# Deformable layer beside a state-space scan: the scan's preparation in bank 2, lower weights in SBUF, state rows issued in a tile's second slot

## The chip, the core and the metric

The kernel runs on one core of one Trainium2 chip. The metric is device time in microseconds of one execution. The five engines are named as in the profile: PE (matmul; PEld its weight loads), DVE (vector), ACT (scalar), POOL (GpSimd) and SP, which here only issues DMAs. The kernel divides PSUM into eight tiles of 128 x 512 float32, called banks below.

## What is computed

Four residual layers over a batch of four images of 128 channels by 128 x 128 pixels, in float32, each behind a group norm:

```
x = x + deformable_conv(gn(x))     # offsets and mask from a 3x3 conv, bilinear samples, 9 taps
x = x + dilated_conv_chain(gn(x))  # 5x7 conv, two 1x1
x = x + state_space_block(gn(x))   # layer norm, projections, a scan in four directions, gate
x = x + central_difference_conv(gn(x))
```

Two parts matter here. The deformable layer samples each of nine taps at a computed place, as a weighted sum of four neighbours, and multiplies by a 128 x 128 matrix:

```
sampled = (corner(y0, x0, (1-ly)*(1-lx)) + corner(y0, x0+1, (1-ly)*lx)
         + corner(y0+1, x0, ly*(1-lx)) + corner(y0+1, x0+1, ly*lx)) * mask
out = einsum('bckhw,ock->bohw', sampled, weight)
```

The scan runs, for each of four directions, 128 channels and 16 states, along all 16384 pixels:

```
h = h * exp(delta * A) + (delta * u) * B
y = einsum('bkcn,bkn->bkc', h, C)
```

## The kernel before

**Two streams.** The program is written as Python generators. `scan` is the main stream: 512 tiles t (4 images x 4 directions x 32 blocks of 512 pixels). `together` draws a side stream beside it: for each scanned image the end of the image before (`layer2_post`, `layer3`) and the start of the next (`layer0_table`, `layer0`, `layer1`, `layer2_pre`), so that each side step comes at a fixed share of the scan's steps. The first image's `layer0` runs alone, the last stretch has no `layer0`: three of the four runs of `layer0` stand beside the scan. `keep_order` then fixes the written order of instructions on every engine, so what is issued early or late is decided in the Python text.

**A scan tile.** A tile has four parts j of four scans g, 16 slots. For each j, `inputs` multiplies du by the state rows into h (L936; on DVE the rows come from the PSUM tile dub, which `states_up`, L929, makes by a matmul; on POOL from an SBUF tile bb), `decay` makes exp(delta * A) on ACT into a PSUM tile pa (L966), L1079 is the scan on DVE, `carry_on` (L997) keeps the last column, `outputs` (L1003) multiplies h by cb, and `sums` (L977) adds up over states by matmul into yacc, which `finish` copies out and stores. While `layer0` runs beside it (`beside["busy"]` is "POOL"), all four inputs and all outputs are on DVE, otherwise the outputs and one input are on POOL.

**Preparation.** `prepare(t + 2)` is a generator drawn once a slot through `more` (three or four times in a part j). It makes three PSUM tiles, pdt, pxbc and psum, a chain of ACT instructions, delta and, on POOL, du (L908), and stores both to DRAM, from where they are spread over partitions.

**PSUM.** Four banks are the scan's: dub, two pa and yacc. Four are the side's: bank0 to bank3. In `layer0`, bank 0 holds the output sums acc (L510), banks 1 and 3 alternate for the transposed samples pst (L490), bank 3 serves the positions of the next strip while `got["third"]` is set, and bank 2 holds wl, the weights of the lower two neighbours. Where the side leaves bank 3 free (`beside["spare"]`, all other stages), the scan owns it: `own` is true, preparation's tiles lie in it, and a third pa when no preparation is under way. Beside `layer0`, `own` is false and preparation shares the one dub bank with the state rows.

**The deformable layer's weave.** Its unit n is a block of 512 pixels and a tap, 288 an image. `gather(n)` issues four indirect DMAs on POOL (L447) of 128 rows of 2 KB, and one POOL multiply of an earlier unit (L455). Two units later, ACT weighs the upper neighbours (L468) and DVE the lower ones, `weigh_lower`, two instructions L479 a unit; PE transposes and adds the four neighbours into pst (L490), ACT copies it to smp (L502), PE projects (L510), DVE adds the residual (L517). `positions` (L359 to L420) is drawn once a unit by `look` for the next strip of four blocks, and `lower_weights` makes wl once a strip (L428).

Of the kernel before, what the change touches and what calls it, by code (L numbers as in the profile page):

```python
# [10 lines left out]
F32 = mybir.dt.float32  # L11
# [7 lines left out]
P = 128  # L19
# [4 lines left out]
N = R * W  # L24
NBLK = H // R
KK = 9
# [5 lines left out]
NG = 4  # L32
# [8 lines left out]
ROWS = 16  # L41
# [71 lines left out]
def conv_preact_kernel(ctx: ExitStack, tc: tile.TileContext, a: dict, nb: int):  # L113
    nc = tc.nc
# [5 lines left out]
    pss = ctx.enter_context(tc.tile_pool(name="scps", bufs=1, space=PSUM))  # L120
# [7 lines left out]
    def bank(which, name):  # L128
        return psb.tile([P, N], F32, name=name, tag=f"bank{which}")

    waiting = []
    beside = {}
# [179 lines left out]
    def layer0(st, pairs=10):  # L312
# [5 lines left out]
        with ExitStack() as s:  # L318
# [6 lines left out]
            mp = s.enter_context(tc.tile_pool(name="l0m", bufs=1))  # L325

            got = {}
# [9 lines left out]
            def positions(j):  # L337
# [4 lines left out]
                y0 = j * ROWS  # L342
                xs, base, top = got["s", j]

                got["third"] = True
                po = bank(3, "po")
                po3 = po.rearrange("p (r w) -> p r w", w=W)
# [76 lines left out]
            def lower_weights(j):  # L424

                wts = got.pop(("l", j))
                wl = bank(2, "wl")[:, 0 : 2 * ROWS * KK]
                nc.vector.tensor_mul(  # L428
                    wl.rearrange("p (q n) -> p q n", q=2),
                    wts[:, 1:2, 0].to_broadcast([P, 2, ROWS * KK]), wts[:, :, 1],  # L430
                )
                got["p"] = wl.rearrange("p (q r b k) -> p r b k q", q=2, r=R, b=BPS)
# [105 lines left out]
                yield None  # L538
            flush()
            beside["full"] = True  # L540
            while beside.get("own") or beside.get("third"):
                yield None
            fetch_strip(0)
            for n, _ in enumerate(positions(0)):
# [6 lines left out]
                yield share + (1.0 - share) * f  # L551
            flush()
            beside["full"] = False
        st["x1"], st["stats1"] = keep, stats_out


# [260 lines left out]
    def scan(pull):  # L817
# [4 lines left out]
        seq = []  # L822
# [30 lines left out]
        def prepare(t, early=False):  # L853

            st, k, i, back = seq[t]
            c = blocks[t]
            if (st["b"], k) not in carries:
                carries[st["b"], k] = carry = small.tile([P, NST], F32, name="carry")
                nc.vector.memset(carry, 0.0)
            c["carry"] = carries[st["b"], k]  # L860
            c["bc"] = st["bc"][k % 2][i, k // 2]
            u = c["u"]
            own = beside.get("own")
            beside["prepares"] = own

            def place(name):
                return bank(3, name) if own else pss.tile([P, N], F32, name=name, tag="dub")

            yield None
            if own:  # L870
                yield None
            pdt = place("pdt")
            nc.tensor.matmul(pdt, wd[:, k, :], u, start=True, stop=True)
            yield None

            dtb = col(V_DTB + k)
            e = sp.tile([P, N], F32, name="e", bufs=1)
            nc.scalar.activation(e, pdt, AF.Abs, bias=dtb)
            above = sp.tile([P, N], F32, name="above", bufs=1)
            nc.scalar.activation(above, pdt, AF.Relu, bias=dtb)  # L880
            yield None
            nc.scalar.activation(e, e, AF.Exp, scale=-1.0)
            yield None
            one_e = sp.tile([P, N], F32, name="one_e", bufs=1)
            nc.scalar.activation(one_e, e, AF.Identity, bias=1.0)
            yield None
            if not back:
                px = place("pxbc")
                nc.tensor.matmul(px, xbc[:, k, :], u, start=True, stop=True)
            ln = sp.tile([P, N], F32, name="ln", bufs=1)  # L890
            nc.scalar.activation(ln, one_e, AF.Ln)
            yield None
            if not back:
                bc = sp.tile([4 * NST, N], F32, name="bc", bufs=1)
                nc.scalar.copy(bc, px[0 : 4 * NST])  # L895
                store(st["bc"][k][i].rearrange("d j s t -> (d j s) t"), bc)
            nc.scalar.activation(one_e, one_e, AF.Identity, bias=minus)  # L897
            yield from slots(1 if own else 2 if early else 4)
            pd = place("psum")
            for n, (t, sign) in enumerate(((e, ident), (one_e, less), (ln, ident), (above, ident))):  # L900
                nc.tensor.matmul(pd, sign, t, start=n == 0, stop=n == 3)  # L901
            yield from slots(1 if early else 2)
            steps = sp.tile([P, 2, N], F32, name="steps", bufs=1)
            delta, du = steps[:, 0, :], steps[:, 1, :]
            nc.scalar.copy(delta, pd)  # L905
            beside["prepares"] = False
            yield from slots(2 if early else 1)
            nc.gpsimd.tensor_mul(du, delta, u)  # L908
            c["steps"] = sd = dram.tile([P, 2 * N], F32, name="stepsd", bufs=4)
            store(sd, steps.rearrange("p j t -> p (j t)"), 2)  # L910
# [14 lines left out]
        def states_up(t, j):  # L925

            c = blocks[t]
            c["pb", j] = p = pss.tile([P, N], F32, name="dub", tag="dub")
            nc.tensor.matmul(p, xb[:, seq[t][1], j, :], c["u"], start=True, stop=True)  # L929
# [22 lines left out]
        def decay(n):  # L952

            t, n = divmod(n, NST)
            j, g = divmod(n, NG)
            k = seq[t][1]
            turn = (ahead["turn"] + 1) % 3
            if turn == 2 and (not beside.get("own") or beside.get("prepares")):
                turn = 0
            ahead["turn"] = turn  # L960
            if turn == 2:
                beside["third"] = beside.get("third", 0) + 1
                blocks[t]["third", n] = True
            pa = bank(3, "pa3") if turn == 2 else pss.tile([P, N], F32, name="pa", bufs=2)
            at = g * NG + j
            nc.scalar.activation(pa, blocks[t]["d", g], AF.Exp, scale=neg_a[:, k, at : at + 1])  # L966
            blocks[t]["a", n] = pa
# [54 lines left out]
        for t, (st, k, i, back) in enumerate(seq):  # L1022
            c = blocks[t]
            carry = c["carry"]
            on_vector = beside.get("busy") == "POOL"
            own = beside["own"] = bool(beside.get("spare")) and not beside.get("full")
            c["by"] = nc.vector if on_vector else nc.gpsimd
            more = prepare(t + 2, on_vector) if t + 2 < len(seq) else iter(())
            if t > 0:
# [1 line left out]
            for j in range(NG):  # L1031
# [16 lines left out]
                for g in range(NG):  # L1048
                    n = j * NG + g
                    if g == 1:  # L1050
                        decays(at + 1)
                        if t + 1 < len(seq) and j == 3:
                            spread_steps(t + 1, 2)
                            spread_steps(t + 1, 3)
                        if t + 1 < len(seq) and j == (2 if c["by"] is nc.gpsimd else 3):
                            spread_products(t + 1)
                        next(more, None)
                        if before[0] >= 0:
                            carry_on(*before, c["by"])
                            outputs(*before, c["by"])  # L1060
                        if earlier[0] >= 0 and not own:
                            sums(*earlier)
                        if own and j == 2 and t > 0:
                            finish(t - 1)
                    if n and g in (0, 3):
                        next(more, None)
                    if g == 3 and not own and then[0] < len(seq) and not (then[1] == NG - 1 and c["by"] is nc.gpsimd):
                        states_up(*then)
                    if g == 2:
                        decays(at + 2)  # L1070
                        if j == 0 and c["by"] is nc.gpsimd:
                            inputs(t, NG - 1, nc.gpsimd)
                        next(more, None)
                        if own and then[0] < len(seq) and not (then[1] == NG - 1 and c["by"] is nc.gpsimd):
                            states_up(*then)
                    o, f = h[:, g, :], c["a", n]
                    if back:
                        o, f = o[:, ::-1], f[:, ::-1]
                    nc.vector.tensor_tensor_scan(o, f, o, carry[:, n : n + 1], ALU.mult, ALU.add)  # L1079
                    if ("third", n) in c:  # L1080
                        beside["third"] -= 1
                    if g == 3:
                        decays(at + 3)
                        if own and earlier[0] >= 0:
                            sums(*earlier)
                        if not own and j == 1 and t > 0:
                            finish(t - 1)
                    yield (t * NST + n + 1) / total
            for _ in more:
                pass  # L1090
        t = len(seq) - 1
# [422 lines left out]
```

## Time and profile before

| what | us |
|---|---|
| median of 3 runs (20785.77 to 20800.34) | 20786.91 |
| the profiled execution, its own time | 20838.75 |
| its span, from the first to the last instruction | 20837.0 |
| gathers alone, first image (217 to 1930) | 1713 |
| gathers beside the scan (3446 to 5309, 8625 to 10443, 13537 to 15356) | 1863, 1818, 1819 |

Busy time of each engine in some stretches, from the trace:

| stretch, us | PE | DVE | ACT | POOL |
|---|---|---|---|---|
| 217 to 1930 (1713) | 1048.80 | 434.35 | 740.46 | 1288.72 |
| 3446 to 5309 (1863) | 1434.60 | 1645.09 | 1227.41 | 1540.28 |
| 8625 to 10443 (1818) | 1356.92 | 1438.83 | 1146.39 | 1488.65 |
| 13537 to 15356 (1819) | 1372.55 | 1434.63 | 1146.43 | 1488.93 |
| 5330 to 8570 (3240) | 2622.91 | 3036.56 | 2164.35 | 2799.78 |
| 10470 to 13500 (3030) | 2487.29 | 2824.51 | 2033.41 | 2567.93 |

How to read profile lines: a group's line gives the source line, engine, operation, output<-input by the program's names, shapes and count; then its busy time in us and the mean of one in ns; then the engine's idle time just before these instructions and what ended it. "issue" means that the profile shows nothing that the engine waited for. In order of time a line gives start, length, engine, line, operation, and in brackets the idle time before it. Small gaps between POOL's instructions are not counted as busy.

### The profile page before, as it was taken

To read this page: it belongs to the slowest core of one execution; us is meant where nothing else is said; L and a number is where in the kernel's file an instruction comes from. 1 tells how busy PE (TensorE), PEld (TensorE's weight loads), DVE (VectorE), ACT (ScalarE), POOL (GpSimd) and SP (SyncE) were. 2 spreads that over 40 slices of the span, in tenths; PEclk is the share of its full clock that TensorE was granted. 3 is DMA by queue.
4 is the path that set the end of the run, shared out by engine and by line. 5 is a ranking of instruction groups with operands and counts; after the bars stand their busy time and mean duration, and the time that the engine had idled before them with its cause. 6 is when DMAs were issued, how large, how long until landed. Compare 5 with 4: busy or idle time off the path is not lost.

```text
span 20837.0 us, 209864 instructions
## 1 busy us (share of the span) xinstructions
PE 15847.0 (76%) x58778; PEld 6719.5 (32%) x58778; DVE 16855.7 (81%) x14665; ACT 12887.2 (62%) x25086; POOL 16827.5 (81%) x10597
## 2 busy tenths in 40 slices
PE   4667776777878888777778887877777877677778
PEld 2444222444322223344422222244432222122223
DVE  1222588888999899888899889978889998999983
ACT  3444566666667666566667776666666767655563
POOL 4775577888788888888878888888878889999994
PEclk7888888998989999899999998988998988899899
DMA  7666678777767877777777796777776777555673
GB/s 234 192 193 191 193 229 283 259 255 253 245 205 225 235 236 254 239 247 251 247 235 224 225 250 229 253 244 248 248 241 221 235 216 221 185 185 195 197 219 120
DMA packets 2909354, 4717.50 MB, mean 226 GB/s; under 512 B 1095248, under 2 KB 1369240, under 8 KB 2831264
## 3 DMA queue, kind: packets, MB, share of 16 engines
q1 hardware_dynamic: 2539552, 3495.83, 52.5%
q0 software_dynamic: 368640, 1208.25, 18.8%
q8 instruction: 476, 7.80, 0.1%
q14 instruction: 686, 5.62, 0.1%
HBM read 3766.27 MB, written 908.60 MB: 224 GB/s over the span
## 4 chain that ended last, share of the span: by engine, by line
DVE 34%; PE 19%; issue 12%; DMA 11%; ACT 10%; POOL 8%; another core or an unknown queue 3%; SPq 2%; DVEq 0%; POOLq 0%; ACTq 0%
DVE h L1079 20%; DVE h L936 11%; PE pst L490 4%; PE psum L901 4%; POOL g L447 3%; DMA du<-stepsd 3%; ACT pa L966 3%; DMA g<-table,idx 2%; PE acc L510 2%; ACT g L468 2%; DMA delta<-stepsd 2%; PE p L1309 1%; POOL h L1003 1%; PE yacc L977 1%
## 5 line engine op out<-in xcount | busy, mean ns | idle before, releaser
L1079 DVE TENSOR_TENSOR_SCAN h<-pa,carry,h 128x512 f32<-128x512 f32 x8192 | 10005.1, 1267 | 767.6 <-ACT pa L966 571.5
L966 ACT ACTIVATE pa<-delta,neg_a 128x512 f32<-128x512 f32 x8192 | 5538.0, 687 | 4751.5 <-DVE h L1079 3700.4
L1003 POOL TENSOR_TENSOR h<-h,cb 128x2048 f32<-128x2048 f32 x1692 | 7670.5, 4533 | 137.0 <-POOL carry L997 0.6
L447 POOL DMA_INDIRECT g<-table,idx x4608 | 4874.2, 1058 | 1679.5 <-issue 1136.4
L936 DVE TENSOR_TENSOR h<-du,dub 128x2048 f32<-128x2048 f32 x1625 | 3684.3, 2267 | 826.4 <-PE dub L929 310.3
L490 PE MATMUL pst<-ident,g 128*128 128x128 f32 x18432 | 2670.0, 299 | 1665.1 <-issue 644.8
L929 PE MATMUL dub<-u,xb_sb 128*128 128x512 f32 x3250 | 2047.3, 716 | 1713.3 <-DVE h L936 1529.8
L490 PEld LDWEIGHTS pst<-ident,g 128*128 128x128 f32 x18432 | 2312.0, 155 | 2699.8 <-issue 1297.6
L468 ACT ACTIVATE g<-g,wt 128x128 f32<-128x128 f32 x8072 | 2577.6, 392 | 216.7 <-DMA g<-table,idx 162.4
L977 PE MATMUL yacc<-h,gather_sb 128*32 128x512 f32 x16384 | 2364.6, 650 | 87.0 <-POOL h L1003 61.0
L936 POOL TENSOR_TENSOR h<-du,bb 128x2048 f32<-128x2048 f32 x423 | 1927.4, 4557 | 18.1 <-DMA du<-stepsd 18.1
L479 DVE TENSOR_TENSOR g<-g,wl 128x512 f32<-128x512 f32 x2304 | 1488.2, 669 | 359.9 <-DMA g<-table,idx 315.4
L502 ACT COPY smp<-pst 128x512 f32<-128x512 f32 x1152 | 664.8, 577 | 1569.9 <-remote 1013.2
L929 PEld LDWEIGHTS dub<-u,xb_sb 128*128 128x128 f32 x3250 | 598.4, 210 | 2877.1 <-DVE h L936 2211.9
L510 PE MATMUL acc<-smp,w_sb 128*128 128x512 f32 x2304 | 1371.3, 679 | 133.2 <-DVE x L517 60.9
L908 POOL TENSOR_TENSOR steps<-steps,u 128x512 f32<-128x512 f32 x512 | 652.5, 1274 | 909.5 <-ACT steps L905 905.2
L1309 PE MATMUL p<-xn,w_l_sb 128*128 128x508 f32 (+2 forms) x2304 | 1149.6, 620 | 1.8 <-ACT xn L1288 1.8
L977 PEld LDWEIGHTS yacc<-h,gather_sb 128*32 128x32 f32 x16384 | 338.3, 112 | 1838.1 <-issue 1315.9
L901 PE MATMUL psum<-e,ident 128*128 128x512 f32 x1024 | 613.8, 684 | 357.6 <-ACT bc L895 338.0
L901 PE MATMUL psum<-one_e,less 128*128 128x512 f32 x1024 | 639.1, 711 | 310.7 <-ACT one_e L897 310.1
L517 DVE TENSOR_TENSOR x<-acc,xres 128x512 f32<-128x512 f32 x128 | 87.1, 680 | 966.5 <-remote 525.3
L455 POOL TENSOR_SCALAR g<-g,wt 128x128 f32<-128x128 f32 x1144 | 833.0, 728 | 37.4
(170 smaller groups left out, 18122.0 us busy)
## 6 DMA issues: line engine op xcount, KB each, us to landing
cb<-bcd SPq DMA_DIRECT2D x512, 1024.0 KB
delta<-stepsd SPq DMA_DIRECT2D x2048, 256.0 KB
du<-stepsd SPq DMA_DIRECT2D x2048, 256.0 KB
stepsd<-steps SPq DMA_DIRECT2D x512, 512.0 KB
table<-gt SPq DMA_DIRECT2D x512, 256.0 KB
bb<-bcd SPq DMA_DIRECT2D x512, 256.0 KB
win<-nd SPq DMA_DIRECT2D x512, 160.0 KB
g<-table,idx POOLq DMA_INDIRECT x4608
```

The costliest lines, as they stand in the source:

```text
L447: nc.gpsimd.indirect_dma_start(out=g[:, r].rearrange("p q c -> p (q c)"), out_offset=None, in_=table, in_offset=bass.IndirectOffsetOnAxis( ...
L468: nc.scalar.activation(g, g, AF.Copy, scale=w)
L479: nc.vector.tensor_mul(g, g, wl.unsqueeze(3).to_broadcast([P, 2, 2, P]))
L490: nc.tensor.matmul(pst[:, r * P : (r + 1) * P], g[:, r % 2, q, :], ident, start=q == 0, stop=q == 3, is_transpose=True,)
L510: nc.tensor.matmul(got["a", i], w0[:, k, :], got.pop(("c", n)), start=k == 0, stop=k == KK - 1)
L901: nc.tensor.matmul(pd, sign, t, start=n == 0, stop=n == 3)
L929: nc.tensor.matmul(p, xb[:, seq[t][1], j, :], c["u"], start=True, stop=True)
L936: engine.tensor_mul(h, c["du"], b.unsqueeze(1).to_broadcast([P, NG, N]))
L966: nc.scalar.activation(pa, blocks[t]["d", g], AF.Exp, scale=neg_a[:, k, at : at + 1])
L977: nc.tensor.matmul(c["y"][g * Q : (g + 1) * Q, :], gather, c["h", j][:, g, :], start=j == 0, stop=last and not second,)
L1003: engine.tensor_mul(h, h, c["cb"][:, j, :].unsqueeze(1).to_broadcast([P, NG, N]))
L1079: nc.vector.tensor_tensor_scan(o, f, o, carry[:, n : n + 1], ALU.mult, ALU.add)
```

## The change

Four edits belong together. `lower_weights` puts wl into an SBUF tile of the pool `mp` instead of bank 2. `own` becomes a number: 3 where the scan owns bank 3, 2 beside `layer0` (then preparation's tiles lie in bank 2), 0 otherwise; `beside["prepares"]` is now set at the start of each tile, and the third pa is allowed only where `own` is 3. Where `own` is 2, `states_up` for the next part comes in the second slot (g 1), after preparation's step, instead of the fourth; as `own` is true there now, `sums` and `finish` take the places that they have in the other stages. And `layer0` waits at its end until a preparation in bank 2 is through, and, where `positions` takes bank 3, first copies out the transposed samples that are still in a bank.

```diff
@@ positions
+                for n in [key[1] for key in got if key[0] == "t" and isinstance(key, tuple)]:
+                    copy(True)(n)
                 got["third"] = True
                 po = bank(3, "po")
@@ lower_weights
                 wts = got.pop(("l", j))
-                wl = bank(2, "wl")[:, 0 : 2 * ROWS * KK]
+                wl = mp.tile([P, 2 * ROWS * KK], F32, name="wl")
@@ layer0
-            while beside.get("own") or beside.get("third"):
+            while beside.get("own") == 3 or beside.get("third"):
                 yield None
...
             flush()
             beside["full"] = False
+            while beside.get("own") == 2 and beside.get("prepares"):
+                yield None
@@ prepare
             def place(name):
-                return bank(3, name) if own else pss.tile([P, N], F32, name=name, tag="dub")
+                return bank(own, name) if own else pss.tile([P, N], F32, name=name, tag="dub")
@@ decay
-            if turn == 2 and (not beside.get("own") or beside.get("prepares")):
+            if turn == 2 and (beside.get("own") != 3 or beside.get("prepares")):
                 turn = 0
@@ scan
-            own = beside["own"] = bool(beside.get("spare")) and not beside.get("full")
+            own = beside["own"] = 2 if beside.get("full") else 3 if beside.get("spare") else 0
+            beside["prepares"] = own if t + 2 < len(seq) else 0
...
                         next(more, None)
+                        if own == 2 and then[0] < len(seq):
+                            states_up(*then)
                         if before[0] >= 0:
...
-                        if own and then[0] < len(seq) and not (then[1] == NG - 1 and c["by"] is nc.gpsimd):
+                        if own == 3 and then[0] < len(seq) and not (then[1] == NG - 1 and c["by"] is nc.gpsimd):
                             states_up(*then)
```

## The prediction

> **What bounds the kernel now.** I read the page's head first, then the busy times by stretch, then the groups by line inside the one kind of stretch that the diff touches, and last the order of time there on two engines. The profiled execution took 20838.75 us (span 20837.0). The runs shown have a median of 20786.91, 0.25% less, so I work out a difference in the profiled execution and add it to the median.
>
> ```profile
> span 20837.0 us, 209864 instructions
> PE 15847.0 (76%) x58778; PEld 6719.5 (32%) x58778; DVE 16855.7 (81%) x14665; ACT 12887.2 (62%) x25086; POOL 16827.5 (81%) x10597
> ```
>
> No engine is full on average, so the share says little and the stage must be read. The gathers of L447 mark the deformable layer: they run from 217 to 1930 us alone, and beside the scan from 3446 to 5309, 8625 to 10443 and 13537 to 15356 us, three stretches of 1863, 1818 and 1819 us. Between them DVE is busy 3037 of 3240 us (5330 to 8570): the scan's engine is the bound there. In the gathers' stretches it is not: DVE 1439 of 1818. The groups of 8900 to 10300 us, 1400 us from the middle of such a stretch, tell who is:
>
> ```profile
> L447 POOL DMA_INDIRECT g<-table,idx x885 | 961.7, 1087 | 242.9 <-issue 198.7 <-ACT g L468 7.2 <-DVE g L479 6.6
> ...
> L479 DVE TENSOR_TENSOR g<-g,wl 128x512 f32<-128x512 f32 x445 | 290.1, 667 | 51.8 <-DMA g<-table,idx 40.5 <-issue 10.9
> ...
> L1003 DVE TENSOR_TENSOR h<-h,cb 128x2048 f32<-128x2048 f32 x84 | 196.6, 2341 | 2.9
> L936 DVE TENSOR_TENSOR h<-du,dub 128x2048 f32<-128x2048 f32 x83 | 189.6, 2285 | 180.6 <-PE dub L929 53.8 <-issue 44.4 <-remote 33.7
> L455 POOL TENSOR_SCALAR g<-g,wt 128x128 f32<-128x128 f32 x221 | 166.3, 753 | 7.3
> ...
> L908 POOL TENSOR_TENSOR steps<-steps,u 128x512 f32<-128x512 f32 x21 | 26.8, 1276 | 0.0
> ```
>
> Add POOL up: 961.7 + 242.9 + 166.3 + 7.3 + 26.8 = 1405 of 1400 us (the ends overlap). The 242.9 us are 885 gaps of 0.27 us, each 0.30 us between two gathers or 0.17 after a multiply: POOL's own pace, not a wait. Gaps longer than that add only 1, 7 and 8 us in the three stretches. **POOL is full beside the scan**, and nobody makes it wait. DVE's 180.6 us ahead of L936, where it waits for PE's state rows, is time that POOL hides.
>
> Now why a gather has a mean of 1087 ns where its median is 949. POOL, then DVE, in order of time (start, length, engine, line):
>
> ```profile
> 9518.79 1.02 POOL L447 DMA_INDIRECT g<-table,idx  x1 [0.16 <-issue]
> ...
> 9522.64 2.98 POOL L447 DMA_INDIRECT g<-table,idx  x1 [0.30 <-issue]
> ...
> 9536.86 2.74 POOL L455 TENSOR_SCALAR g<-g,wt 128x128 f32<-128x128 f32 x1
> ```
>
> ```profile
> 9518.13 2.29 DVE L936 TENSOR_TENSOR h<-du,dub 128x2048 f32<-128x2048 f32 x1 [11.03 <-remote]
> ...
> 9522.50 2.29 DVE L1003 TENSOR_TENSOR h<-h,cb 128x2048 f32<-128x2048 f32 x1
> ...
> 9536.91 2.29 DVE L1003 TENSOR_TENSOR h<-h,cb 128x2048 f32<-128x2048 f32 x1
> ```
>
> L1003 and L936 have the same shape and length. L1003 reads two SBUF tiles, and each time the POOL instruction that starts under it is about 2 us longer, a gather (2.98) or a multiply (2.74). L936 has one input in PSUM, and the gather under it keeps its 1.02. So a DVE instruction with **both inputs in SBUF** holds up the POOL instruction that starts under it. In the stretch the held time is 885 x (1087 - 949) ns + 221 x (753 - 624) ns = 150.6 us, less 13 us for the first gather after a multiply (221 x 0.06): 137 us over 84 L1003, **1.64 us each**. L479 does not do it today: its wl lies in PSUM.
>
> **The change, part by part.**
>
> *wl moves from bank 2 to SBUF.* L428 and L479 keep their number (576 of L479 for each of four images) and length (row L1003 against L936: 2341 and 2285 ns, the same within 56 ns). But L479 now has two SBUF inputs, like L1003. Its price is POOL time. The starts show the rule to use: a gather that began before the DVE instruction isn't held, one that begins under it ends 0.83 us after it, that is 0.12 us of its 0.95 are done by then. An instruction of 0.667 us so holds for about 0.52 us; POOL starts five instructions in a group of 5.58 us (four gathers, one multiply); with starts at random the mean hold is 5 / 5.58 x 0.52 squared / 2 = 0.12 us. The same sum for L1003 (2.13 us less 0.57, the mean time to the next start) gives 1.56 against 1.64 measured. So 576 x 0.12 x 1.05 = 73 us an image is one end. The other: laying L479's recorded intervals over POOL's recorded starts, with what L1003 already holds kept, POOL grows by 42 to 59 us in a stretch as recorded, and by 23 to 56 if DVE is stretched by 2 to 6% against it. I take 50, since L479 often sits next to an L1003 that has held POOL already: **3 x 50 = +150 us** (69 to 219).
>
> The Trainium skill, "SBUF — State Buffer", section "Who interferes with whom", speaks against this part: a DVE instruction with two SBUF inputs contends with a GpSimd one that reads SBUF, and whoever comes second blocks fully. The L1003 rows agree on the block (2.98 against 0.95 us). Read as if every L479 cost POOL its whole length, that is 576 x 0.667 x 3 = +1150 us; the starts above say that most L479 fall between two POOL starts.
>
> *The same in the first image's layer, alone.* There POOL is less full: 1110.4 + 179.0 us busy, and 102 us of its gaps in 1700 are longer than its pace, since it also waits for buffers and landings. The replay gives 48 to 66 us; those waits can take up part or all. I take **+30** (0 to 66).
>
> *The scan's preparation gets bank 2 (own is 2), state rows come at g 1 instead of g 3, sums and finish move two or more slots later.* No instruction is added and no DMA: one matmul pair (x166 for 83 rows) moves up, four sums by four matmuls move down, finish and its store by SP move from tile 1's last to tile 2's second slot, so one 256 KB store goes past a few loads in SP's queue; its reader is a later direction, many blocks off. pdt and the pair after it come a slot later, psum, delta and L908 in the same slots as now, so POOL's multiply of the steps isn't later. What goes away is PE's and DVE's wait about the dub bank (53.8 + 44.4 us in 1400). POOL hides it: **0**. If POOL's cover were gone this would be worth up to the 180.6 us of the row, or some 235 us a stretch; that is rival one. At each edge of a stretch POOL stands some 30 us (30.3 to 34.2 before the first gather, waiting for idx), of which a freer PE may save a few: **-10** (0 to -60, which takes the 1 + 7 + 8 us of gaps in).
>
> *The early copies when positions start.* A copy moved up inside its step, seven times an image, on ACT, busy 1146 of 1818: 0, at most 7 x 0.58 us x 3 = 12 if PE's waiting were bare.
>
> *The third decay bank.* "prepares" is now set at a tile's start, not at its second scan. Only decays 1 and 2 of a tile could lose bank 3. Counting turns: after nine alternating decays the cycle puts the third bank at decays 13 and 16 of a tile, and these stay allowed. So the scan's other stages keep their order: 0, with 50 either way if the cycle settles elsewhere (a tenth of the 528 us that DVE waits for pa outside the gathers).
>
> *The wait at the layer's end.* The next layer may start up to 11 scan slots later, some 35 us at 16 slots in 50 us, three times. DVE, the bound there, goes on scanning meanwhile and the side work catches up at double rate: **+10**, and 105 if DVE has to idle for it.
>
> Sum: +150 + 30 + 0 - 10 + 10 = **+180 us**, so 21019 us profiled and **20967 us** at the median.
>
> **Rivals.**
> 1. *The bank was the bound.* For it: DVE idles 180.6 us in 1400 ahead of L936, mostly for PE. If half of 235 us a stretch came home, 3 x 118 = 353 less: 20787 - 353 + 30 = 20464, **faster**. Against: POOL's 1405 of 1400. It decides from the point where POOL's waits beyond its pace exceed what L479 adds (50 us a stretch); now they are 1 to 8. 7%.
> 2. *wl's second read doesn't hold POOL*, for L479's inner dimension repeats one weight 128 times and no row has that shape. Then only the edges and waits are left: 20787 + 0, **within 0.2%**. For it: the 288-element instructions of the positions with two SBUF inputs add only about 0.04 us each. Against: that is what the sum gives for a hold of 0.3 us (0.9 x 0.09 / 2). 11%.
> 3. *The collisions are not random*: L479 comes in pairs, and follows landings that POOL itself paces. If each held POOL for 0.3 us, 576 x 0.3 x 3 = 518, plus 60 alone: 21365. Against: the replay at the recorded phase. 5%.
>
> **How the numbers follow.** The forecast's case has 77%, its own range +50 to +310 (69 + 0 - 30 + 10 to 219 + 66 + 0 + 25). Below it lie rival two and one (18%), above it rival three (5%). The range that leaves two in ten out: 20800 to 21150. A measurement of this kernel tells about 0.2%, 42 us, from no change. Slower by more: 77 + 5 = 82%; within: 11%; faster: 7%.
>
> **What would show it.** Beside the scan, L447's mean up from 1087 by 40 to 80 ns and L455's up too, with gathers of 1.2 to 1.5 us that start under an L479; the three stretches some 1910, 1865 and 1865 us; L936's wait for dub down to near nothing and DVE's idle time put elsewhere; L1079's stretches between them unchanged at about 3240 and 3030 us. Wrong if the gathers keep 1087, if POOL shows waits beyond its pace of over 50 us a stretch, or if the stretches between move by more than 50.

## The result and the profile after

| | before | after |
|---|---|---|
| median, us | 20789.72 (4 runs) | 21063.71 (4 runs) |
| ratio | | 1.0133, 95% interval 1.0121 to 1.0145 |
| span of the profiled execution | 20837.0 | 21081.8 |

The change makes the kernel 274 us slower; +180 was forecast. The lines of the new kernel have moved: the gathers are L449 (L447 before), POOL's multiply L457 (455), the lower weighing L481 (479), the outputs L1007 (1003), the inputs L940 (936), the scan L1086 (1079).

The first and last gather of each image cut both profiled executions into stretches, by which the 244.8 us between the spans can be placed:

| stretch | before | after | difference |
|---|---|---|---|
| gathers of the first image, alone | 1713.0 | 1682.8 | -30 |
| to the next | 1515.8 | 1527.1 | +11 |
| gathers beside the scan, 1 | 1863.0 | 1957.1 | +94 |
| to the next | 3316.1 | 3316.0 | 0 |
| gathers beside the scan, 2 | 1818.8 | 1896.5 | +78 |
| to the next | 3092.9 | 3090.1 | -3 |
| gathers beside the scan, 3 | 1820.2 | 1901.2 | +81 |
| to the end | 5480.3 | 5494.0 | +14 |

More than all of it, 253 us, lies in the three stretches in which the deformable layer stands beside the scan. The +11 and +14 are no more than the spread of these two stretches over all the kernels of this document (1513 to 1536 and 5476 to 5495 us). The groups by line of the new kernel, in the same 1400 us as in the prediction (8900 to 10300 us), POOL's and then DVE's:

```profile
L449 POOL DMA_INDIRECT g<-table,idx x847 | 969.4, 1144 | 230.5 <-issue 174.0 <-DMA g<-table,idx 9.6 <-ACT g L470 8.5
L457 POOL TENSOR_SCALAR g<-g,wt 128x128 f32<-128x128 f32 x212 | 170.1, 802 | 6.9
L912 POOL TENSOR_TENSOR steps<-steps,u 128x512 f32<-128x512 f32 x20 | 25.5, 1277 | 0.0
```

```profile
L481 DVE TENSOR_TENSOR g<-g,wl 128x512 f32<-128x512 f32 x423 | 295.7, 707 | 228.1 <-DMA g<-table,idx 205.5 <-issue 17.5 <-PE acc L512 3.2
L1007 DVE TENSOR_TENSOR h<-h,cb 128x2048 f32<-128x2048 f32 x80 | 183.6, 2295 | 2.8
L940 DVE TENSOR_TENSOR h<-du,dub 128x2048 f32<-128x2048 f32 x79 | 180.0, 2278 | 6.9 <-PE dub L933 6.9
```

Three things are to be seen. POOL is as full as before (969.4 + 230.5 + 170.1 + 6.9 + 25.5 = 1402 of 1400 us), but it gets through 847 gathers where it had done 885: one takes 1144 ns, not 1087, and a multiply 802, not 753. DVE no longer waits for the state rows: 6.9 us ahead of L940 where there were 180.6. And what it saved there it now spends waiting for gathers to land, ahead of L481: 228.1 us where there were 51.8. **The bank did what it was to do, and POOL, the bound, became slower.**

A fourth is easily missed: L481 itself takes 707 ns where L479 took 667. The wait goes both ways. DVE, then POOL:

```profile
9906.09 2.27 DVE L481 TENSOR_TENSOR g<-g,wl 128x512 f32<-128x512 f32 x1
```

```profile
9905.93 0.63 POOL L457 TENSOR_SCALAR g<-g,wt 128x128 f32<-128x128 f32 x1
9906.52 1.29 POOL L912 TENSOR_TENSOR steps<-steps,u 128x512 f32<-128x512 f32 x1
```

Here POOL was first and keeps its usual lengths, and the weighing that starts 0.16 us behind the multiply takes 2.27 us, past the end of both. In the three stretches 98 of the 1722 weighings start under one of these two POOL instructions and take over 50 ns more than 667, together 52 us. DVE, which waits 228.1 us for gathers anyway, has room for that.

I added up how much longer than its usual 949 (1010 after a multiply) or 624 ns each POOL instruction was, and which DVE instruction with two SBUF inputs lay over it. In the three stretches before: 209, 165 and 166 us under L1003, 2 to 4 under L479. After: 187, 150 and 159 under L1007, **106, 90 and 89 under L481**, 11 to 14 under both. The sum grows by 93, 83 and 87 us, which is the stretches' 94, 78 and 81.

### The profile page after: what moved, and what is told of

Same layout as the page of the kernel before. It is cut to its first block, busy times and chain, and to the rows that moved or that the text cites. A ratio compares the mean times of both kernels' runs of the same rounds, so it can differ in the third digit from the quotient of the medians.

```text
span 21081.8 us, 210018 instructions
## 1 busy us (share of the span) xinstructions
PE 15942.2 (76%) x58778; PEld 6748.2 (32%) x58778; DVE 16990.8 (81%) x14665; ACT 12920.3 (61%) x25086; POOL 17153.0 (81%) x10597
## 4 chain that ended last, share of the span: by engine, by line
DVE 32%; PE 18%; DMA 14%; issue 12%; POOL 10%; ACT 9%; SPq 2%; another core or an unknown queue 2%; DVEq 0%; POOLq 0%; ACTq 0%
DVE h L1086 19%; DVE h L940 10%; POOL g L449 6%; DMA g<-table,idx 6%; PE psum L905 4%; DMA du<-stepsd 3%; PE pst L492 3%; ACT pa L970 3%; PE acc L512 2%; DMA delta<-stepsd 2%; PE p L1316 1%; POOL g L457 1%; ACT g L470 1%; PE yacc L981 1%
## 5 line engine op out<-in xcount | busy, mean ns | idle before, releaser
L1086 DVE TENSOR_TENSOR_SCAN h<-pa,carry,h 128x512 f32<-128x512 f32 x8192 | 10008.7, 1267 | 834.7 <-ACT pa L970 625.9
L1007 POOL TENSOR_TENSOR h<-h,cb 128x2048 f32<-128x2048 f32 x1692 | 7673.1, 4535 | 137.1 <-POOL carry L1001 1.0
L449 POOL DMA_INDIRECT g<-table,idx x4608 | 5167.2, 1121 | 1581.0 <-issue 1000.6
L940 DVE TENSOR_TENSOR h<-du,dub 128x2048 f32<-128x2048 f32 x1625 | 3683.6, 2267 | 206.8 <-DMA du<-stepsd 113.7
L481 DVE TENSOR_TENSOR g<-g,wl 128x512 f32<-128x512 f32 x2304 | 1604.4, 708 | 1469.8 <-DMA g<-table,idx 1259.8
L940 POOL TENSOR_TENSOR h<-du,bb 128x2048 f32<-128x2048 f32 x423 | 1927.4, 4557 | 17.5 <-DMA du<-stepsd 17.5
L512 PE MATMUL acc<-smp,w_sb 128*128 128x512 f32 x2304 | 1433.6, 709 | 87.4 <-issue 50.3
L457 POOL TENSOR_SCALAR g<-g,wt 128x128 f32<-128x128 f32 x1144 | 861.2, 753 | 37.6
L1007 DVE TENSOR_TENSOR h<-h,cb 128x2048 f32<-128x2048 f32 x356 | 816.6, 2294 | 12.2
```

The source lines that it names most:

```text
L449: nc.gpsimd.indirect_dma_start(out=g[:, r].rearrange("p q c -> p (q c)"), out_offset=None, in_=table, in_offset=bass.IndirectOffsetOnAxis( ...
L481: nc.vector.tensor_mul(g, g, wl.unsqueeze(3).to_broadcast([P, 2, 2, P]))
L512: nc.tensor.matmul(got["a", i], w0[:, k, :], got.pop(("c", n)), start=k == 0, stop=k == KK - 1)
L940: engine.tensor_mul(h, c["du"], b.unsqueeze(1).to_broadcast([P, NG, N]))
L1007: engine.tensor_mul(h, h, c["cb"][:, j, :].unsqueeze(1).to_broadcast([P, NG, N]))
```

## The experiments

Each kernel was timed beside the kernel before on the same chip. The chips differ (medians of before from 20790 to 20829), so ratios to before are compared; a stretch's length is from each kernel's one profiled execution.

**wl alone.** The kernel before, with one line of the change:

```diff
-                wl = bank(2, "wl")[:, 0 : 2 * ROWS * KK]
+                wl = mp.tile([P, 2 * ROWS * KK], F32, name="wl")
```

> The kernel before with one edit: wl in SBUF. Theory (L479, now with two SBUF inputs, holds POOL about 0.15 us each; everything else in the change beside the scan is hidden under POOL): the three stretches of gathers beside the scan grow as in the changed kernel, by 94, 78 and 81 us to some 1955, 1895 and 1900, and the first image's, alone, by about 50 from 1713 to 1765, since the early copies are not in; total about +300 us, 21090. Rival (the new order of sums, finish and state rows, or the sharing of bank 2, costs part of it): the three stretches grow by half or less, total +150 or less.

Measured: 1.0122 (1.0105 to 1.0139), the same as the whole change. The stretches beside the scan are 1948, 1902 and 1896 us, and the hold under L479 is 107, 89 and 85. DVE's wait for the state rows, which the whole change took away, is still there (8900 to 10300 us):

```profile
L936 DVE TENSOR_TENSOR h<-du,dub 128x2048 f32<-128x2048 f32 x78 | 178.2, 2285 | 211.7 <-PE dub L929 130.1 <-issue 49.5 <-PE acc L510 14.2
```

So within the intervals the slowdown is wl's place and nothing else; the bank for the preparation, the early rows and the later sums are together worth nothing here that can be told, though they take 211.7 us of DVE's waiting down to 6.9. The first image's stretch was 1703, not 1765: the holds are there (53 us), but POOL's own longer waits shrank from 102 to 41 us.

**The early copies alone.** The kernel before with the two lines ahead of `got["third"] = True` in `positions`.

> The kernel before with one edit: the copies of the transposed samples ahead of the positions. Theory (they free bank 3 before the positions' matmuls ask for it, so PE and behind it the gathers no longer stand for up to 25 us at each strip of the first image): the first image's stretch falls from 1713 to about 1630, the three beside the scan stay at 1863, 1818 and 1819 since POOL is full there; total about -80 us, 20710. Rival (the first stretch became shorter because wl left PSUM): no change, 20790.

Measured: 1.0001 (0.9991 to 1.0010), first stretch 1708, the others 1862, 1819 and 1818. A miss: PE's waits for the copied samples, up to 25 us, which I had made responsible, cost the first image nothing that can be told. The rival that wl's leaving PSUM shortened it has no better footing (1703 with wl alone). In the six kernels with wl in SBUF and POOL's multiply in place the first stretch is 1683 to 1711, in the two with wl in PSUM 1713 and 1708. The kernel of the next experiment has the same instructions in the same order on each engine there as the changed kernel, and took 1707 us where that took 1683. So 24 us of this stretch come and go with the execution, and its -30 is not a measure of the change.

**State rows in the third slot.** The changed kernel with `states_up` back at g 2 for both kinds of `own`:

```diff
-                        if own == 2 and then[0] < len(seq):
-                            states_up(*then)
...
-                        if own == 3 and then[0] < len(seq) and not (then[1] == NG - 1 and c["by"] is nc.gpsimd):
+                        if own and then[0] < len(seq) and not (then[1] == NG - 1 and c["by"] is nc.gpsimd):
```

> The changed kernel with the state rows in the third slot (g 2), as in the other stages, instead of the second. Theory (beside the scan POOL is the bound, so where PE makes the rows is worth nothing): within 25 us of the changed kernel, 21064. Rival (the early rows save DVE time that reaches the end): 60 us or more slower.

Measured: 1.0117 (1.0100 to 1.0133). No difference from the changed kernel's 1.0133 (1.0121 to 1.0145), though DVE's wait ahead of L940 is back at 41.7 us in the same 1400: against the third slot the second is worth nothing while POOL is full.

**The weighing cut in two.** The changed kernel with two instructions of half the length:

```diff
-                nc.vector.tensor_mul(g, g, wl.unsqueeze(3).to_broadcast([P, 2, 2, P]))
+                for r in range(2):
+                    nc.vector.tensor_mul(g[:, r], g[:, r], wl[:, r].unsqueeze(2).to_broadcast([P, 2, P]))
```

> The changed kernel with each lower weighing (128x512, 0.67 us) cut into two of 128x256. Theory (a POOL instruction is held only if it starts under the DVE instruction, until its end, so the mean hold goes with the square of the length): the hold in a stretch beside the scan halves from some 90 to 45 us, the first image's from 53 to 27; total about -160 us against the changed kernel, 20900. Rival (the hold goes with the total time that DVE reads two SBUF inputs): no gain, 21064 or, with 576 more instructions an image on DVE, slightly more.

Measured: 1.0079 (1.0062 to 1.0095), a gain of 0.5%, some 110 us, over the changed kernel. The hold falls to 61, 60 and 62 us a stretch, from 106, 90 and 89. DVE reads two SBUF tiles for no less time in all, so the hold does not go with total time; it goes down with the length of one instruction, though to two thirds rather than half. One reason is that half the shape isn't half the time, 433 ns against 667:

```profile
L482 DVE TENSOR_TENSOR g<-g,wl 128x256 f32<-128x256 f32 x857 | 340.5, 433 | 161.4 <-DMA g<-table,idx 123.6 <-issue 34.2 <-PE pst L493 1.2
```

By the prediction's formula, with 0.15 us taken off each length, two such pieces hold 2 x 0.28 squared / 0.52 squared = 0.58 of what one did (an estimate); measured, 61 of 95 on average is 0.64.

**cb in the bank instead of wl.** wl in SBUF, and ACT copies the part of cb that the next outputs need into bank 2:

```diff
-            engine.tensor_mul(h, h, c["cb"][:, j, :].unsqueeze(1).to_broadcast([P, NG, N]))
+            b = c["cp", j] if engine is nc.vector and ("cp", j) in c else c["cb"][:, j, :]
+            beside["staged"] = False
+            engine.tensor_mul(h, h, b.unsqueeze(1).to_broadcast([P, NG, N]))
...
+        def stage(t, j):
...
+            c = blocks[t]
+            beside["staged"] = True
+            c["cp", j] = p = bank(2, "cbp")
+            nc.scalar.copy(p, c["cb"][:, j, :])
```

(`stage` runs behind the fourth scan of a part, only beside `layer0`, which waits at its end until "staged" is clear.)

> The kernel before with wl in SBUF, and bank 2, free now, takes one part of cb at a time: beside the deformable layer ACT copies cb for part j there (0.58 us, four a tile), and the outputs on DVE (L1003, 2.29 us) read cb from PSUM, so that they have one SBUF input. Theory (the hold comes from the second SBUF input, whatever the instruction): the holds of 1.6 us under L1003 vanish, 209, 165 and 166 us a stretch in the kernel before, while wl's come in without those that L1003 put in step (some 63 us a stretch): stretches of about 1715, 1715 and 1715, the first of them perhaps more as DVE is busy 1645 there; total about -250 to -350 against before, 20440 to 20540. Rival (the copies through one bank make DVE or ACT wait, or the long gathers were not DVE's doing): the stretches stay at 1820 or more, total 20790 or above.

Measured: 0.9977 (0.9968 to 0.9987), the stretches 1858, 1790 and 1777. The mechanism is shown: with cb in PSUM, POOL is held for less than 4 us a stretch under the same multiply of 2.29 us alone, in place of 150 to 209 (14 to 18 more lie under it and a weighing together). The size is a miss. DVE's groups, 8900 to 10200 us:

```profile
L938 DVE TENSOR_TENSOR h<-du,dub 128x2048 f32<-128x2048 f32 x79 | 180.4, 2284 | 179.6 <-PE dub L931 70.3 <-PE acc L510 41.0 <-PE pst L490 34.0
L1007 DVE TENSOR_TENSOR h<-h,cbp 128x2048 f32<-128x2048 f32 x78 | 178.4, 2287 | 8.1
```

Once POOL had time, DVE's wait for PE was bare: 179.6 us in 1300 ahead of L938, 70.3 of them for the rows in the shared dub bank, and POOL itself now waits 99, 46 and 42 us a stretch beyond its pace. That these waits set the time there is argued from the trace, not tested. And the holds under L479 stayed at 89, 84 and 79, where I had expected 63; why stays open.

**A memset ahead of the weighing.** The changed kernel with an instruction more on DVE, whose result nobody reads:

```diff
                     g = got["g", n, h][:, :, 2:4, :]
+                    nc.vector.memset(mp.tile([P, P], F32, name="pad"), 0.0)
```

> The changed kernel with one DVE instruction more ahead of each lower weighing, a memset of 128x128 of some 0.2 us that nobody reads. Theory (a held gather ends 0.83 us after the DVE instruction and the next starts 0.30 us on, and a scan between takes about 1.2 us, so that the next lower weighing starts just ahead of or with the gather and holds it in full; 0.2 us later it starts behind the gather): the holds at the very start of L481, 53 of 0.52 us a stretch, go, and the kernel is 50 to 100 us faster than the changed one although DVE has some 110 us a stretch more to do. Rival (the phases are random, or the memset itself holds POOL): the same time or slower.

Measured: 1.0089 (1.0072 to 1.0106), 0.44% of the kernel before's time, or some 90 us, less than the changed kernel, with more work. First, in the changed kernel, what it is to break: DVE and POOL in order of time.

```profile
9605.12 2.29 DVE L1007 TENSOR_TENSOR h<-h,cb 128x2048 f32<-128x2048 f32 x1
9607.33 1.28 DVE L1086 TENSOR_TENSOR_SCAN h<-pa,carry,h 128x512 f32<-128x512 f32 x1
9608.53 0.67 DVE L481 TENSOR_TENSOR g<-g,wl 128x512 f32<-128x512 f32 x1
```

```profile
9606.31 1.93 POOL L449 DMA_INDIRECT g<-table,idx  x1 [0.30 <-issue]
9608.54 1.47 POOL L449 DMA_INDIRECT g<-table,idx  x1 [0.30 <-remote]
```

L1007 ends at 9607.41 and holds the gather of 9606.31, which ends 0.83 us later, at 9608.24; the next starts 0.30 on, at 9608.54. DVE makes one scan after L1007 and starts L481 at 9608.53. The two start within 10 ns of each other, and the gather is held for its full 0.52 us (1.47 for 0.95). The scan's step of 1.2 us and POOL's 0.83 + 0.30 agree, so a hold can put the next one in place. In the changed kernel 133, 102 and 95 of some 575 weighings a stretch have a POOL start within 60 ns before or after their own. With the memset it is 48, 47 and 50, about the number that random starts would give (575 x 0.12 us x the 0.77 starts per us of that trace = 53), and the hold under the weighing is 71, 73 and 69 us, not 106, 90 and 89. A weighing whose last POOL instruction was held by an L1007 has, in the mean over the three stretches of the changed kernel, a hold of 0.51 us under it; one behind a POOL instruction that was not held 0.15. DVE's groups with the memset:

```profile
L482 DVE TENSOR_TENSOR g<-g,wl 128x512 f32<-128x512 f32 x426 | 284.3, 667 | 185.5 <-DMA g<-table,idx 148.1 <-issue 28.6 <-PE pst L493 4.5
...
L480 DVE MEMSET pad<- 128x128 f32 x426 | 70.3, 165 | 0.0
```

**POOL's multiply given to ACT.** In four kernels the multiply L455 is left to ACT with the other upper weighings:

```diff
-                    if h == 1 and n >= 2:
-                        g, w = neighbour(n - 2, h, 1, 1)
-                        nc.gpsimd.tensor_scalar(g, g, w, None, ALU.mult)
...
-                            if h == 1 and r == 1 and c == 1 and n + 2 < NBLK * KK:
-                                continue
```

> The kernel before with POOL's multiplies of the deformable layer (L455, one a unit) given back to ACT, so that POOL only gathers. Theory (beside the scan POOL is the bound and its time is the sum of its starts plus what DVE holds): 288 units of 4 x 1.25 us, 33 to 41 us of L908 and 165 to 209 us of holds make 1645 to 1690 us a stretch; DVE, busy 1645 in the first and 1440 in the others, and PE's shared dub bank come next, so some 1800, 1730 and 1730, total about -240, 20575. Rival (with POOL out of the way the waits for the dub bank take its place at once): 1840, 1800 and 1800, total -40.

> The changed kernel with the same multiplies given to ACT. Theory (POOL with L481's holds of some 100 us a stretch more: 1790, 1735, 1735, and no waits for dub, since preparation has bank 2): total about -250 against before, 20565. Rival one of the prediction (the bank is worth something once POOL isn't the bound): faster than the kernel before with the same edit by 30 us or more although POOL has more to carry. Rival (L481's holds cost as before and the bank nothing): slower than that kernel by 150 us or more.

> The kernel with cb and wl exchanged (cb's part in bank 2, wl in SBUF) with the same multiplies given to ACT. POOL's own sum falls to about 1590, far under DVE's 1648 in the first stretch. Theory (in that kernel the bound has already gone over to PE's shared dub bank and DVE): little is gained over it, 1840, 1760 and 1760 us a stretch, total about -90 against before. Rival (POOL is still its bound): 1700, 1620 and 1620, total -500.

> The changed kernel with the multiplies given to ACT and each lower weighing cut into two of 128x256. Theory (the holds fall by some 35 us a stretch, as the cut did without ACT's help, and POOL is still the bound of the two later stretches): about -90 us against the same kernel uncut. Rival (POOL no longer is the bound): no difference, or up to 30 us slower by DVE's 576 more instructions an image.

| kernel, with the multiply on ACT | ratio to before | stretches beside the scan, us |
|---|---|---|
| the kernel before | 0.9990 (0.9981 to 1.0000) | 1842, 1777, 1789 |
| the changed kernel | **0.9963** (0.9949 to 0.9977) | 1827, 1787, 1774 |
| cb in the bank | 1.0011 (1.0001 to 1.0020) | 1887, 1770, 1785 |
| the changed kernel, weighing cut in two | 0.9968 (0.9955 to 0.9980) | 1791, 1770, 1774 |

The kernel before gains almost nothing: rival right. The changed one gains 1.7% on itself and beats both kernels, and the kernel before with the same edit by 0.27%, the intervals apart: more than the 30 us that rival one asks for, though some 77 us under the kernel before and not the 250 of the theory. POOL's and DVE's groups in 8900 to 10200 us tell why. The kernel before with the multiply on ACT:

```profile
L447 POOL DMA_INDIRECT g<-table,idx x842 | 910.1, 1081 | 342.7 <-issue 219.8 <-ACT g L463 28.9 <-ACT smp L497 25.9
...
L931 DVE TENSOR_TENSOR h<-du,dub 128x2048 f32<-128x2048 f32 x79 | 180.5, 2284 | 175.2 <-PE dub L924 68.2 <-PE pst L485 37.4 <-remote 28.0
```

The changed kernel with it on ACT:

```profile
L449 POOL DMA_INDIRECT g<-table,idx x834 | 990.3, 1187 | 275.5 <-issue 202.7 <-ACT g L465 15.7 <-DMA g<-table,idx 8.5
...
L935 DVE TENSOR_TENSOR h<-du,dub 128x2048 f32<-128x2048 f32 x78 | 177.7, 2278 | 7.7 <-remote 2.5 <-PE dub L928 2.3 <-PE pdt L872 1.8
```

In the first, POOL idles 342.7 us; its pace of 0.305 us explains 842 x 0.305 = 257, so it waits 86 us, with DVE waiting 175.2 ahead of L931: nobody is full. In the second POOL waits 275.5 - 254 = 21 us although a gather has a mean of 1187 ns, and DVE waits 7.7. What the change does beside wl's move is worth something as soon as POOL has room, which it never had in the two kernels compared. These two kernels differ in all of the change at once, so how much of it is the bank and how much the earlier rows, later sums and early copies is not shown. Cutting the weighing then gives nothing in all (0.9968 against 0.9963), a miss for its theory: in the profiled executions the stretches beside the scan are 53 us shorter, and the first image's is 27 us longer. Nor does exchanging cb and wl go with ACT's help, a miss too: with 1362 us of work in a first stretch of 1887, ACT now has the multiply and the copies, and POOL waits up to 11.5 us for the steps from ACT. Whether that is the cause stays open.

> The changed kernel with the multiplies given to ACT and the same memset ahead of each lower weighing. Theory (there POOL is a little short of being the bound and DVE has less slack): the same as without the memset, 0.996 of before, within 30 us either way. Rival (POOL's holds still decide): 60 us faster than without it.

Measured: 0.9955 (0.9938 to 0.9971), the same as without the memset, as expected. The holds under the weighing fall (135, 112 and 106 us a stretch without the memset, 39, 50 and 51 with it), and POOL's waits beyond its pace grow from 15, 41 and 42 to 135, 111 and 97 us: there POOL's holds no longer decide alone.

## Why the prediction was right, step by step

- **POOL is full beside the scan, and what PE and DVE save is worth nothing.** Right, and the step that decided. The 180.6 us ahead of L936 fell to 6.9 and nothing of it that can be told came home (wl alone, with 211.7 us of that wait, 1.0122, whole change 1.0133).
- **wl's hold, +150 us.** The mechanism was right, the term mis-sized: 94 + 78 + 81 = 253 us, above its upper end of 219. A weighing costs 0.15 us, not 0.087. The step that failed is the choice between the two ends: "I take 50, since L479 often sits next to an L1003 that has held POOL already". Being next to L1003 makes it worse, since the hold lines POOL's next start up with the next weighing. The replay missed it because its rule for the first instant, which had been read off L1003 (a gather that starts up to 46 ns after the beginning of L1003 is not held), let exactly these gathers through. The trace before has the coincidences already: 92, 83 and 97 weighings a stretch with a POOL start within 60 ns. Laid over its recorded starts again, without any shifts, the weighings give 59 to 61 us a stretch with the rule of 46 ns and 92, 87 and 94 without it (estimates), against 94, 78 and 81 measured. The formula for random starts, 73 us, was the nearer end: with the memset, which takes the lock step away, the hold is 69 to 73 us. But L1003 is not all of it: with cb in the bank, and so without L1003's holds, the hold under the weighing was still 79 to 89 us.
- **L479 keeps its length.** Not quite: 707 for 667 ns, since the weighing now waits for POOL's multiplies. The 56 ns between L1003 and L936, which the prediction counted as the same length, were such waits: most L1003 take 2.29 us, two of the 84 took 3.97. POOL hid this too.
- **The first image, +30.** Measured -30 in the changed kernel, -11 to -2 in others with wl in SBUF, with a spread of 24 us between two executions of the same instructions. The holds of 53 us are in the trace, so the replay's 48 to 66 was right; POOL's waits beyond its pace fell from 102 to 20 us (to 41 with wl alone) and took all of it up and more.
- **The early copies 0, the third decay bank 0, the layer's end +10, the edges -10.** Right within what can be told: the copies alone 1.0001, the stretches between the gathers 0 and -3 us, POOL's wait before the first gather 33.8, 30.5 and 30.8 us against 34.2, 30.4 and 30.3.
- **Rival one** (the bank was the bound) is wrong for these kernels and right in kind once POOL's multiply is taken off, 0.9990 against 0.9963, at some 55 us where it had 353. **Rival two** (wl's second read doesn't hold POOL) is refuted by wl alone. **Rival three** (collisions are not random) was right in kind: they are not, but they cost 0.15 us each, not 0.3.
- **The sum, +180.** Between the profiled spans 245 were measured: 103 more for wl's term, 60 less for the first image, 22 more in the rest. That the total came so near is in part luck, as the second miss makes up for much of the first.

The Trainium skill's "SBUF — State Buffer", section "Who interferes with whom", had the rule that decided the sign: two SBUF inputs on DVE contend with GpSimd's reads, one doesn't. Both halves are shown here, by wl moved into SBUF (2 to 4 us of hold become 85 to 107) and by cb moved out of it (150 to 209 fall below 4). It says that the one that comes second blocks. The trace agrees for a POOL multiply that comes first (2.27 us for the weighing behind it), but a gather that is already under way when the DVE instruction starts was not held, and did not hold it either: 922 of 958 such weighings in the three stretches stay within 50 ns of 667.

## What to carry to other kernels

Look first at which engine is full in the stretch that a change touches: a freed bank, or an instruction moved earlier, was worth nothing beside a full engine, and the same edit paid once that engine had room. Where DVE and POOL work side by side, a tile's place (PSUM or SBUF) is part of the schedule: a DVE instruction's second SBUF input was paid by POOL, and the longer the instruction the more (0.15 us under one of 0.67 us, 1.64 under one of 2.29). And when two engines' cadences agree, collisions repeat; place them by the recorded starts, and take the rule for the first instant from more than one kind of instruction.

## What had not been expected of the hardware

- A hold of POOL by DVE fixes the phase of what follows. One scan (1.2 us a step) and the rest of a held gather plus its gap (0.83 + 0.30 us) are so near each other that a quarter to a sixth of the weighings met a POOL start within 60 ns, about twice as many as at random, and a DVE instruction of 165 ns that does nothing made the changed kernel 0.4% faster.
- An indirect gather on POOL was held only near its start: of 0.95 us, about 0.12 are done when it is stopped, and one that began some 50 ns before the DVE instruction or earlier runs through at its usual length. Under L1003 the same held for one that began up to 46 ns after it, under L481 not.
